# Layer 1 of a four-layer graph network: another order of the last block's turn, the partial products and the sums on TensorE and VectorE

## The chip, the cores and the metric

The kernel runs on one core of a Trainium2 chip. The metric is the device time of one execution in microseconds (us). Times of engines come from one profiled execution. The engines named here are PE (TensorE, matrix products; its weight loads are shown apart, as PEld), DVE (VectorE), ACT (ScalarE), POOL (GpSimd) and SP (SyncE, which issues the transfers). [...]

## The reference

A network with 512 nodes, 512 features and 16384 edges has four layers; each one normalises its input, cuts it at zero, and adds the layer's result to `x`:

```python
edge_index = jnp.stack([src, dst])
h = jnp.maximum(_layernorm(x, axis=-1), 0.0)
x = x + _L0_gnn_ref(h, edge_index, ...)      # attention over the graph, feed-forward
h = jnp.maximum(_layernorm(x, axis=-1), 0.0)
x = x + _L1_gnn_ref(h, L1_gnn_wc, L1_gnn_wn, L1_gnn_bias, edge_index)
h = jnp.maximum(_layernorm(x, axis=-1), 0.0)
x = x + _L2_gnn_ref(h, ...)                  # four experts of two layers, the best two per node
h = jnp.maximum(_layernorm(x, axis=-1), 0.0)
x = x + _L3_gnn_ref(h, edge_index, L3_gnn_W, L3_gnn_b)
```

The change lies in layer 1:

```python
alpha = x @ wc
beta = x @ wn
src, dst = (edge_index[0], edge_index[1])
sums = jax.ops.segment_sum(beta[dst], src, num_segments=x.shape[0])
counts = jax.ops.segment_sum(jnp.ones_like(src, dtype=beta.dtype), src, num_segments=x.shape[0])
gamma = sums / counts[:, None]
return alpha + gamma + bias
```

## The kernel before

The nodes are four blocks of 128 rows. The edges are counted into a 512 x 512 matrix once (`CT`, and `C` the other way round), so that a sum over neighbours is a matrix product with it. `xs` holds the residual stream, `h` the normalised rows, `hT` the same turned round. A *turn* of block b (`turn`, L189; `turn_pe`, L855) is four transposes on TensorE and one copy on ScalarE into `hT`.

Layer 1 (L870 to L974) does the following.

- *alpha*: `alpha_mm(b)` (L835) is four fp32 matmuls of 128 x 512 into the bank `pal`, which the profile shows as eight records. The function it returns adds the bank to `xs` on VectorE (L838). `add_bias1(b)` (L832) adds the bias to `xs` before it.
- *beta* = h · wn as a product of two 2 x 2 matrices of quarters with seven products instead of eight. `product(p, i, B)` (L778) is the i-th, four matmuls (eight records) of 128 x 256. Its operands are quarters of `hT` and `wns`, and sums of quarters that VectorE makes: `ls[0]` to `ls[3]` for `hT` (L749 to L752), `rb[0]` to `rb[3]` for `wns` (L759 to L762). Product 4 needs `ls[0]` and `rb[0]`, product 5 `ls[1]` and `rb[1]`, product 6 `ls[2]` and `rb[2]`, product 3 `rb[3]`, product 2 `ls[3]`; 0 and 1 need none, and no row of block 2 or 3.
- Three banks collect them: `pbe_a` takes products 0 and 1, `pbe_b` 5, 6 and 3, `pbe_c` 4 and 2. They go on adding into the same bank, and VectorE reads the state in between: `u2` after product 5, `u3` after 6, a third sum after 3 (all `plus`, L787, on L789). So product 6 can't start before `u2` has read `pbe_b`, nor product 3 before `u3` has.
- `beta_quarter` (L829) writes a quarter of beta as two parts: a rounded one by ScalarE (L726), and the rest by VectorE (`lo00` to `lo11`, L727).
- `gamma_mm(b)` (L840) is the sum over the neighbours, eight matmuls over the four blocks j of beta and its two parts; VectorE scales it and adds it to `xs` (L843). Then block b is normalised on VectorE and ScalarE (`gamma_begin`, `gamma_end`), turned, and used for the gates (`gates_mm`) and for layer 2's neighbour sums (`around_mm`, banks `pag`).
- `f0[0]` to `f0[7]` are VectorE's sums of the weights of layer 2's first expert (`wr0_0`, `wl0_0`).

The order on TensorE, VectorE and ScalarE is that of the code between L870 and L974: `manual_schedule` takes it as written. SP's queue of transfers isn't part of it; a load goes out when its place in the pool of five weight tiles is free. [...] a bank is given away again after the last use of what lay in it.

Of the kernel before, what the change touches and what calls it, by code (L numbers as in the profile page):

```python
# [22 lines left out]
NB = N // P  # L23
# [13 lines left out]
def fast(  # L37
# [4 lines left out]
    nc = tc.nc  # L42
# [11 lines left out]
    def bank(name):  # L54
        pool, tag = banks[taken[0] % len(banks)]
        taken[0] += 1
        return pool.tile([P, 512], F32, tag=tag, name=name)
# [73 lines left out]
    h = const.tile([P, NB, D], F32, name="h")  # L131
    hT = const.tile([P, KB, N], F32, name="hT")
# [46 lines left out]
    def norm_relu_end(blocks, name, begun, first=None):  # L179
        rs = rsqrt_end(*begun[1])  # L180
        for i, b in enumerate(blocks):
            nc.scalar.activation(h[:, b, :], begun[0][i], AF.Copy, scale=rs[:, i:i + 1])
            if first is not None:
                nc.scalar.activation(first, begun[0][i], AF.Copy, scale=rs[:, i:i + 1])
# [4 lines left out]
    def turn(dst_t, src_t, b, name):  # L189

        p = bank(f"tp_{name}{b}")
        for k in range(KB):
            nc.tensor.transpose(p[:, k * P:(k + 1) * P], src_t[:, b, k * P:(k + 1) * P], ident)
        nc.scalar.copy(dst_t[:, :, b * P:(b + 1) * P], p.rearrange("p (k n) -> p k n", k=KB))

    def mm(p, pairs):
        for i, (a, c) in enumerate(pairs):
            nc.tensor.matmul(p, a, c, start=(i == 0), stop=(i == len(pairs) - 1))  # L198

    def blk(t, k, j):  # L200
        return t[:, k, j * P:(j + 1) * P]
# [20 lines left out]
    CT = ct_p.tile([P, NB, N], R, name="CT")  # L222
# [187 lines left out]
    def ff_up_mm(hf, f):  # L410

        if f == 0:
            ffT[hf] = ffp.tile([P, FB, W], F32, tag="ffT", name=f"ffT{hf}")
        p = bank(f"pff{hf}_{f}").rearrange("p (i n) -> p i n", i=2)
        for i in range(2):
            mm(p[:, i, :], [(blk(w1[f // 4], k, (f + i) % 4), hT[:, k, hf * W:(hf + 1) * W]) for k in range(KB)])
        return p
# [26 lines left out]
    def norm2_c(b, begun):  # L444
        norm_relu_end((b,), "n1_", begun)
# [34 lines left out]
    with tc.manual_schedule(engines={ET.PE, ET.DVE, ET.Activation}):  # L480
# [25 lines left out]
        for c in range(NCH):  # L506
# [16 lines left out]
            i, at = divmod(c - 17, 9)  # L523
            if 0 <= i < len(first):
                w, t, off, j, cols = first[i]
# [98 lines left out]
        p = ff_up_mm(0, 2)  # L624
# [13 lines left out]
        p = ff_up_mm(0, 6)  # L638
# [39 lines left out]
        p = ff_up_mm(1, 0)  # L678
# [29 lines left out]
        p2, p3 = bank("pf22"), bank("pf23")  # L708
# [15 lines left out]
    def split_hi(hi, lo, full):  # L724

        nc.scalar.copy(hi, full)  # L726
        return lambda: nc.vector.tensor_sub(lo, full, hi.bitcast(F32))  # L727
# [26 lines left out]
    def right_steps(t, s, keep=None):  # L754

        b11, b12, b21, b22 = (quarter(t, i, j) for i in range(2) for j in range(2))
        last = b12 if keep is None else keep
        return (b11, b21, b22, s[:, 2], s[:, 0], s[:, 1], last), [
            lambda: nc.vector.tensor_sub(s[:, 0], b12, b11),  # L759
            lambda: nc.vector.tensor_sub(s[:, 1], b22, s[:, 0]),  # L760
            lambda: nc.vector.tensor_sub(last, b22, b12),
            lambda: nc.vector.tensor_sub(s[:, 2], b21, s[:, 1])]  # L762
# [9 lines left out]
    def right_sums(*a):  # L772
        return all_of(*right_steps(*a))

    def halves(name):
        return bank(name).rearrange("p (m n) -> p m n", m=2)

    def product(p, i, some, fresh=False):  # L778

        for m in range(2):  # L780
            for l, r in some:
                for k in range(2):
                    nc.tensor.matmul(p[:, m, :], l[i][:, k, m * P:(m + 1) * P], r[i][:, k, :], start=fresh,  # L783
                                     stop=(k == 1), skip_group_check=True)
                    fresh = False

    def plus(x, p, y=None):  # L787
        t = uu.tile([P, 2, W], F32, tag="u", name="u_sum") if y is None else y
        nc.vector.tensor_add(t, p, x)  # L789
        return t  # L790
# [21 lines left out]
    def sums_tile(name):  # L812
        return ws.tile([P, 3, 2, W], F32, tag="ws", name=f"ws_{name}")
# [12 lines left out]
    beta = pair.bitcast(R)  # L826
    hs = main.tile([P, 2, NB, D], R, tag="hs", name="hs")

    def beta_quarter(i, j, value):  # L829
        return split_hi(*(beta[:, g, 2 * i:2 * i + 2, j * W:(j + 1) * W] for g in range(2)), value)  # L830

    def add_bias1(b):  # L832
        nc.vector.tensor_add(xs[:, b, :], xs[:, b, :], bias1_b)

    def alpha_mm(b):  # L835
        p = bank(f"pal{b}")
        mm(p, [(blk(hT, k, b), wcs[:, k, :]) for k in range(KB)])
        return lambda: nc.vector.tensor_add(xs[:, b, :], p, xs[:, b, :])  # L838

    def gamma_mm(b):  # L840
        p = bank(f"psu{b}")
        mm(p, [(blk(CT, j, b), beta[:, i, j, :]) for j in range(NB) for i in range(2)])
        return lambda: nc.vector.scalar_tensor_tensor(xs[:, b, :], p, icnt[:, b:b + 1], xs[:, b, :],  # L843
                                                      op0=ALU.mult, op1=ALU.add)

    def gamma_begin(b):
        return norm_relu_begin((b,), "n2_")
# [22 lines left out]
    with tc.manual_schedule(engines={ET.PE, ET.DVE, ET.Activation}):  # L870
        RB, rb = right_steps(wns, sums_tile("wns"))
        ub, last = (uu.tile([P, 2, W], F32, tag="u", name=n) for n in ("u_first", "u_last"))
        L, ls = left_steps(hT, sums_tile("hT"), last)
        B = [(L, RB)]
        w0 = [load_w(src_w[0, 0], nm) for nm, src_w in (("wr0_0", Wr), ("wl0_0", Wl))]
        F0, f0 = zip(*(left_steps(w, sums_tile("w0")) for w in w0))
        f0 = [*f0[0], *f0[1]]
        ba = halves("pbe_a")
        product(ba, 0, B, True)
        nc.scalar.copy(ub, ba)  # L880
        a3 = norm2_a(3, y23)
        al = alpha_mm(0)
        turn(hT, h, 2, "h2_")
        n3 = norm2_b(3, *a3)
        al1 = alpha_mm(1)
        norm2_c(3, n3)
        product(ba, 1, B)
        lo00 = beta_quarter(0, 0, ba)
        add_bias1(0)
        al()  # L890
        rb[0]()
        al2 = alpha_mm(2)
        turn(hT, h, 3, "h2_")
        add_bias1(1)
        al1()
        ls[0]()
        rb[1]()
        ls[1]()
        bb, bc_ = halves("pbe_b"), halves("pbe_c")
        product(bc_, 4, B, True)  # L900
        product(bb, 5, B, True)
        rb[2]()
        ls[2]()
        rb[3]()
        ls[3]()
        add_bias1(2)
        al2()
        u2 = plus(ub, bb)
        product(bb, 6, B)
        lo00()  # L910
        f0[0]()
        u3 = plus(ub, bb)
        product(bb, 3, B)
        lo11 = beta_quarter(1, 1, plus(u3, bc_))
        product(bc_, 2, B)
        f0[1]()
        lo11()
        lo10 = beta_quarter(1, 0, plus(ub, bb))
        f0[2]()
        al3 = alpha_mm(3)  # L920
        lo10()
        lo01 = beta_quarter(0, 1, plus(u2, bc_))
        f0[3]()
        lo01()
        add_bias1(3)
        al3()
        for step in f0[4:6]:
            step()
        pg = bank("pg")
        pag = [bank(f"pag{k}") for k in range(KB)]  # L930
        psu = [gamma_mm(b) for b in range(3)]
        psu[0]()
        g0 = gamma_begin(0)
        psu[1]()
        gamma_end(0, g0)
        g1 = gamma_begin(1)
        cp = turn_pe(0)
        cp()
        psu.append(gamma_mm(3))
        psu[2]()  # L940
        gamma_end(1, g1)
        hs_low(0)
        gates_mm(0)
        g2 = gamma_begin(2)
        cp = turn_pe(1)
        cp()
        around_mm(0)
        psu[3]()
        gamma_end(2, g2)
        hs_low(1)  # L950
        gates_mm(1)
        g3 = gamma_begin(3)
        cp = turn_pe(2)
        cp()
        around_mm(1)
        f0[6]()
        gamma_end(3, g3)
        hs_low(2)
        cp = turn_pe(3)
        cp()  # L960
        f0[7]()
        hs_low(3)
        gates_mm(2)
        around_mm(2)
        gates_mm(3)
        around_mm(3)
        spair = main.tile([P, 2, NB, D], F32, tag="pair", name="sums")
        sums = spair.rearrange("p g s (k n) -> p g s k n", k=2)
        agT = main.tile([P, KB, N], F32, tag="agT", name="agT")
        XR = [right_sums(hT, sums[:, 0, 0:3], sums[:, 0, 3])]  # L970
        for k in range(KB):
            nc.vector.tensor_mul(agT[:, k, :], pag[k], ideg_b)
        XR.append(right_sums(agT, sums[:, 1, 0:3], sums[:, 1, 3]))
        F1 = weights0(1)  # L974
# [613 lines left out]
```

## Time and profile before

| | us |
|---|---|
| median of 3 runs | 522.12 (521.72 to 522.43) |
| the profiled execution | 524.05 |
| its span | 522.3 |
| TensorE busy in the span | 483.4 (93%) |
| VectorE busy | 367.7 (70%) |
| ScalarE busy | 156.9 (30%) |
| layer 1: the first product of beta starts | 208.84 |
| layer 1: the last turn of its input starts | 223.03 |
| layer 1: the last block of alpha starts | 239.88 |
| layer 1: the first neighbour sum is added on VectorE | 245.45 |
| layer 2: the first product starts | 265.11 |

By stage, busy us of each engine in the same execution:

| stretch, us | TensorE | VectorE | ScalarE | granted clock |
|---|---|---|---|---|
| 208.84 to 223.63 | 14.79 | 9.01 | 3.47 | 1.00 |
| 223.63 to 242.91 | 15.21 | 14.50 | 2.44 | 0.82 |
| 242.91 to 259.11 | 14.94 | 14.88 | 7.72 | 1.00 |
| 259.11 to 265.11 | 6.00 | 4.86 | 1.14 | 1.00 |

In an answer in order of time, a row has start and length, engine, line, operation, what is written and what is read (with sizes), how often, and in brackets for how long the engine stood idle before it and which instruction released it. Ends of matmuls are modelled and overlap by up to 0.2 us with the next start; from start to start is the better measure there. In a row by stretches, the numbers after the stretch are its length and then the busy time of PE, PEld, DVE, ACT and POOL, each with its count; the last three are the granted TensorE clock (1.00 is full), the share of the transfer engines, and GB/s.

### The profile page before, as it was taken

The numbers are of one execution on the slowest core, as the hardware profiler recorded it, in microseconds if no ns is written. First come the engines' busy times: TensorE is split into PE (matmuls) and PEld (weight loads), VectorE is DVE, ScalarE is ACT, GpSimd is POOL, SyncE is SP. The second block draws the span as 40 slices with busy tenths as digits, with TensorE's granted clock in tenths as the row PEclk, the third lists the DMA queues.
The fourth block names the chain that finished last, engine by engine and source line by source line (L and its number), as shares of the span: only waits on it lengthen the run. The fifth ranks groups of instructions, "written<-read, shape, count | busy, mean of one in ns | idle before, by whom it ended". The sixth has DMA issues, their size and how long they took to land.

```text
span 522.3 us, 5703 instructions
## 1 busy us (share of the span) xinstructions
PE 483.4 (93%) x2183; PEld 364.4 (70%) x2183; DVE 367.7 (70%) x744; ACT 156.9 (30%) x317; POOL 2.8 (1%) x10
## 2 busy tenths in 40 slices
PE   2999889697999999969999999999999999999995
PEld 1798556354774584547788888888888888885544
DVE  8898999998887784667993627851587135656652
ACT  3886344340531241201601122021112031122443
POOL 2000000000000000000000000000000000000000
PEclk9999999988999999988999999999999999999999
DMA  7810201200002133305000422220422040000002
GB/s 252 294 71 1 80 1 59 103 22 0 1 21 70 51 125 129 129 0 162 0 1 13 149 70 93 80 82 0 162 80 82 0 162 0 2 0 1 1 0 85
DMA packets 18497, 34.41 MB, mean 66 GB/s; under 512 B 1528, under 2 KB 2080, under 8 KB 18464
## 3 DMA queue, kind: packets, MB, share of 16 engines
q1 hardware_dynamic: 17504, 32.47, 18.4%
q10 hardware_dynamic: 960, 1.51, 0.8%
q8 instruction: 19, 0.31, 0.3%
q14 instruction: 14, 0.11, 0.1%
HBM read 32.93 MB, written 1.05 MB: 65 GB/s over the span
## 4 chain that ended last, share of the span: by engine, by line
PE 73%; DVE 20%; ACT 4%; issue 2%; DMA 0%; DVEq 0%; ACTq 0%
PE pe_b L783 8%; PE pff L198 5%; PE pe_a L783 5%; PE pf L430 5%; PE pe_c L783 5%; PE pq L198 5%; PE pz_b L783 3%; PE po_b L783 3%; PE pqk L198 3%; PE pwo L377 3%; PE pal L198 3%; PE ph L198 3%; PE cps L273 2%; DVE m L304 2%; PE po_c L783 2%; PE pz_c L783 2%
## 5 line engine op out<-in xcount | busy, mean ns | idle before, releaser
L789 DVE TENSOR_TENSOR u_sum<-pe_b,u_first 128x512 f32<-128x512 f32 x12 | 8.3, 692 | 50.8 <-PE pe_b L783 50.8
L198 PE MATMUL pq<-zz,C 128*128 128x512 f32 x128 | 32.8, 409 | 0.0
L271 DVE TENSOR_SCALAR ohs<-iota_h,src_f,dw_i 128x256 bf16<-128x256 f16 x104 | 28.9, 341 | 1.7 <-PE cps L273 1.6
L198 PE MATMUL pff<-hT,w 128*128 128x256 f32 x128 | 28.6, 381 | 0.4 <-issue 0.4
L273 PE MATMUL cps<-ohs,ohd 128*128 128x256 bf16 x104 | 19.7, 288 | 10.0 <-DVE ohs L271 10.0
L198 PEld LDWEIGHTS pq<-zz,C 128*128 128x128 f32 x128 | 24.0, 188 | 6.7 <-issue 1.2
L430 PE MATMUL pf<-w,ffT 128*128 128x512 f32 x64 | 28.1, 592 | 0.0
L1040 ACT ACTIVATE re<-te,gt 128x512 f32<-128x512 f32 x16 | 11.6, 724 | 54.9 <-DVE te L1038 54.9
L198 PEld LDWEIGHTS pff<-hT,w 128*128 128x128 f32 x128 | 24.1, 190 | 4.7 <-issue 1.4
L1002 ACT ACTIVATE eT<-u_sum,vecs 128x256 f32<-128x256 f32 x24 | 10.9, 500 | 52.9 <-DVE u_sum L789 52.9
L273 PEld LDWEIGHTS <-ohd 128*128 128x128 f16 x128 | 15.8, 145 | 14.1 <-DVE ohd L266 8.3
L430 PEld LDWEIGHTS pf<-w,ffT 128*128 128x128 f32 x64 | 11.9, 190 | 13.9 <-issue 13.9
L299 PE MATMUL psc<-qT,kT 64*128 64x256 f32 x128 | 17.6, 418 | 4.2 <-DVE s L310 4.2
L304 DVE TENSOR_REDUCE m<-psc 128x256 f32<-128x2048 f32 x8 | 18.3, 2287 | 1.2 <-PE cps L273 1.2
L310 DVE TENSOR_TENSOR s<-psc,m 128x1024 f32<-128x1024 f32 x16 | 18.8, 1216 | 0.1
L348 PE MATMUL aps<-s,v 128*64 128x256 f32 x128 | 16.1, 395 | 3.0 <-DVE nt_l L145 3.0
L726 ACT CAST zz<-u_sum 128x512 fp32r<-128x512 f32 x12 | 7.4, 618 | 37.7 <-DVE u_sum L789 37.7
L299 PEld LDWEIGHTS psc<-qT,kT 64*128 64x128 f32 x128 | 13.3, 204 | 7.8 <-issue 6.5
L338 DVE TENSOR_TENSOR s<-s,r 128x2048 f32<-128x2048 f32 x8 | 18.3, 2286 | 0.1
L311 ACT ACTIVATE s<-s 128x1024 f32<-128x1024 f32 x16 | 16.8, 1054 | 3.3 <-DVE s L310 2.9
L1041 DVE TENSOR_TENSOR xs<-xs,re 128x512 f32<-128x512 f32 x16 | 11.0, 690 | 9.3 <-ACT re L1040 9.3
L789 DVE TENSOR_TENSOR u_sum<-pz_b,u_first 128x512 f32<-128x512 f32 x12 | 8.3, 690 | 11.8 <-PE pz_b L783 11.6
(304 smaller groups left out, 1065.8 us busy)
## 6 DMA issues: line engine op xcount, KB each, us to landing
wr<-in_L_gnn_Wr_dram SPq DMA_DIRECT2D x8, 1024.0 KB
wl<-in_L_gnn_Wl_dram SPq DMA_DIRECT2D x8, 1024.0 KB
w<-in_L_gnn_W_dram SPq DMA_DIRECT2D x5, 1024.0 KB
wk<-in_L_gnn_Wk_dram SPq DMA_DIRECT2D x1, 1024.0 KB
wq<-in_L_gnn_Wq_dram ACTq DMA_DIRECT2D x1, 1024.0 KB
wv<-in_L_gnn_Wv_dram SPq DMA_DIRECT2D x1, 1024.0 KB
wo<-in_L_gnn_Wo_dram SPq DMA_DIRECT2D x1, 1024.0 KB
bl_b<-in_L_gnn_bl_dram SPq DMA_DIRECT2D x4, 256.0 KB
```

Of the source, the lines that this page charges most:

```text
L198: nc.tensor.matmul(p, a, c, start=(i == 0), stop=(i == len(pairs) - 1))
L271: nc.vector.tensor_scalar(ohs, iota_h, src_f[:, c:c + 1], dw_f[:, c:c + 1], op0=ALU.is_equal, op1=ALU.mult)
L273: nc.tensor.matmul(cps, ohd[0][:, :, c % 8], ohs, start=(c == 0), stop=(c == NCH - 1))
L299: nc.tensor.matmul(psc[i][:, 4 * g + j, :], kT[o:o + HD, j, b * P:(b + 1) * P], qT[o:o + HD, j, cols], start=True, stop=True)
L304: nc.vector.tensor_reduce(m, psc[i].rearrange("p h n -> p n h"), axis=AX.X, op=ALU.max)
L310: nc.vector.tensor_sub(s[:, g, :], psc[i][:, g, :], m[:, None, :].to_broadcast([P, 4, W]))
L311: nc.scalar.activation(s[:, g, :], s[:, g, :], AF.Exp, scale=1.0 / 8.0)
L338: nc.vector.tensor_mul(s, s, rz[i].to_broadcast([P, H, W]))
L348: nc.tensor.matmul(aps[hf][j // 2][o:o + HD, j % 2, :], v[:, b, (2 * j + g) * HD:(2 * j + g + 1) * HD], s[:, 4 * g + j, :], start=(b == 0 ...
L430: nc.tensor.matmul(p, ffT[b // 2][:, f, c:c + P], w2[f // 4][:, f % 4, :], start=(f == 0), stop=(f == FB - 1))
L783: nc.tensor.matmul(p[:, m, :], l[i][:, k, m * P:(m + 1) * P], r[i][:, k, :], start=fresh, stop=(k == 1), skip_group_check=True)
L789: nc.vector.tensor_add(t, p, x)
```

## The change

Layer 1's code gets another order; the same arithmetic is done.

- The turn of block 3 (`turn(hT, h, 3, ...)`) moves from behind product 1 and `alpha` block 2 to directly behind `alpha` block 1.
- `rb[0]` and `rb[1]` move ahead of the first bias and `alpha` sums; the sums of blocks 1 and 2 move later.
- Product 5 goes ahead of product 4, `ls[2]` ahead of `rb[2]`, and `rb[3]` and `ls[3]` behind `u2`.
- `alpha` block 2 moves from ahead of the turn to between products 6 and 3. Block 3 stays behind product 2.
- The weight sums `f0[0]` to `f0[3]` come later; `f0[3]` passes from ahead of to behind `alpha` 3's sum.
- `gamma_mm` can do some of the blocks j; the last neighbour sum is done in two halves, j = 0, 1 ahead of the turn of block 0 and j = 2, 3 behind it.

```diff
-    def gamma_mm(b):
-        p = bank(f"psu{b}")
-        mm(p, [(blk(CT, j, b), beta[:, i, j, :]) for j in range(NB) for i in range(2)])
+    def gamma_mm(b, p=None, some=range(NB)):
+        p = bank(f"psu{b}") if p is None else p
+        for j in some:
+            for i in range(2):
+                nc.tensor.matmul(p, blk(CT, j, b), beta[:, i, j, :], start=(j == 0 and i == 0),
+                                 stop=(j == NB - 1 and i == 1))
         return lambda: nc.vector.scalar_tensor_tensor(xs[:, b, :], p, icnt[:, b:b + 1], xs[:, b, :],
                                                       op0=ALU.mult, op1=ALU.add)
...
-        al = alpha_mm(0)
+        al = [alpha_mm(0)]
         turn(hT, h, 2, "h2_")
         n3 = norm2_b(3, *a3)
-        al1 = alpha_mm(1)
+        al.append(alpha_mm(1))
         norm2_c(3, n3)
+        turn(hT, h, 3, "h2_")
         product(ba, 1, B)
         lo00 = beta_quarter(0, 0, ba)
+        rb[0]()
+        rb[1]()
         add_bias1(0)
-        al()
-        rb[0]()
-        al2 = alpha_mm(2)
-        turn(hT, h, 3, "h2_")
-        add_bias1(1)
-        al1()
+        al[0]()
         ls[0]()
-        rb[1]()
         ls[1]()
         bb, bc_ = halves("pbe_b"), halves("pbe_c")
+        product(bb, 5, B, True)
         product(bc_, 4, B, True)
-        product(bb, 5, B, True)
+        ls[2]()
         rb[2]()
-        ls[2]()
+        u2 = plus(ub, bb)
+        product(bb, 6, B)
         rb[3]()
         ls[3]()
-        add_bias1(2)
-        al2()
-        u2 = plus(ub, bb)
-        product(bb, 6, B)
+        al.append(alpha_mm(2))
         lo00()
-        f0[0]()
+        add_bias1(1)
+        al[1]()
         u3 = plus(ub, bb)
         product(bb, 3, B)
         lo11 = beta_quarter(1, 1, plus(u3, bc_))
         product(bc_, 2, B)
+        add_bias1(2)
+        lo11()
+        al[2]()
+        f0[0]()
+        lo10 = beta_quarter(1, 0, plus(ub, bb))
         f0[1]()
-        lo11()
-        lo10 = beta_quarter(1, 0, plus(ub, bb))
-        f0[2]()
-        al3 = alpha_mm(3)
         lo10()
         lo01 = beta_quarter(0, 1, plus(u2, bc_))
-        f0[3]()
+        al.append(alpha_mm(3))
+        add_bias1(3)
         lo01()
-        add_bias1(3)
-        al3()
-        for step in f0[4:6]:
+        f0[2]()
+        al[3]()
+        for step in f0[3:6]:
             step()
         pg = bank("pg")
         pag = [bank(f"pag{k}") for k in range(KB)]
         psu = [gamma_mm(b) for b in range(3)]
+        p3 = bank("psu3")
+        psu.append(gamma_mm(3, p3, (0, 1)))
         psu[0]()
...
         cp = turn_pe(0)
         cp()
-        psu.append(gamma_mm(3))
+        gamma_mm(3, p3, (2, 3))
         psu[2]()
```

## The prediction

> **What bounds the kernel now.** I read the page's first two parts, then the busy time of each engine by stage, then the waits of this stage, its instructions in order of time, the chain that ended last, and the granted clock.
>
> TensorE is the engine that sets the end, and its clock row has a dip near the middle:
>
> ```profile
> span 522.3 us, 5703 instructions
> PE 483.4 (93%) x2183; PEld 364.4 (70%) x2183; DVE 367.7 (70%) x744; ACT 156.9 (30%) x317; POOL 2.8 (1%) x10
> PEclk9999999988999999988999999999999999999999
> ```
>
> Layer 1 is 208.84 to 265 us. From 265 to 480 TensorE is 96 to 100% busy in every 10 us, so whatever time `pe_a`, the first product of layer 2, gains at 265 the end should gain too. In layer 1 TensorE stands still in a few places. The waits of 205 to 265 us (time in all, times, longest):
>
> ```profile
> PE pbe_b L783 <- DVE u_sum L789: 2.7, 2, 1.9
> PE pbe_c L783 <- DVE ws_hT L749: 1.4, 1, 1.4
> PE tp_h L858 <- ACT h L182: 1.3, 2, 0.8
> ```
>
> The instructions in order of time (start, length, engine) show which work is late:
>
> ```profile
> 223.67 0.58 ACT L194 COPY hT<-tp_h 128x512 f32<-128x512 f32 x1 [3.29 <-PE tp_h L193]
> 224.29 0.69 DVE L749 TENSOR_TENSOR ws_hT<-hT 128x512 f32<-128x512 f32 x1 [4.56 <-ACT hT L194]
> 225.03 1.99 PE L783 MATMUL pbe_c<-ws_wns,ws_hT 128*128 128x256 f32 x8 [1.40 <-DVE ws_hT L749]
> ...
> 229.91 0.68 DVE L789 TENSOR_TENSOR u_sum<-pbe_b,u_first 128x512 f32<-128x512 f32 x1
> 230.64 3.06 PE L783 MATMUL pbe_b<-wns,u_last 128*128 128x256 f32 x8 [1.89 <-DVE u_sum L789]
> 233.74 0.69 DVE L789 TENSOR_TENSOR u_sum<-pbe_b,u_first 128x512 f32<-128x512 f32 x1 [1.96 <-PE pbe_b L783]
> 234.49 3.78 PE L783 MATMUL pbe_b<-ws_wns,hT 128*128 128x256 f32 x8 [0.78 <-DVE u_sum L789]
> 239.88 3.60 PE L198 MATMUL pal<-wcs,hT 128*128 128x512 f32 x8
> 243.51 0.69 DVE L838 TENSOR_TENSOR xs<-pal,xs 128x512 f32<-128x512 f32 x1 [0.56 <-PE pal L198]
> 245.45 0.75 DVE L843 SCALAR_TENSOR_TENSOR xs<-psu,icnt,xs 128x512 f32<-128x512 f32 x1
> ```
>
> First, VectorE sat idle 4.56 us until the last turn's copy, and then had ten sums to do at once; TensorE waited 1.40 us for the first (`ls[0]`), 1.89 us for `u2`, which reads the bank that product 6 is about to overwrite, and 0.78 us for `u3`. Second, two products of eight passes took 3.06 and 3.78 us, where their like take 1.89 (product 5 at 226.86). The granted clock, on a grid of 3.41 us laid so that it meets the edges of the clock's drops at 105.1, 125.6 and 231.4 us:
>
> ```profile
> 98.27:101.69 3.42, 1.54 (x12) 1.30 (x12) 3.35 (x5) 0.83 (x2) 0.00 (x0) 1.00 0.74 282
> ...
> 227.98:231.39 3.41, 1.52 (x7) 1.02 (x6) 3.31 (x7) 0.00 (x0) 0.00 (x0) 1.00 0.00 0
> 231.39:234.81 3.42, 2.64 (x7) 1.64 (x6) 1.43 (x3) 0.00 (x0) 0.00 (x0) 0.50 0.00 0
> 234.81:238.22 3.41, 3.41 (x9) 2.69 (x9) 1.64 (x3) 0.62 (x1) 0.00 (x0) 0.50 0.02 5
> ```
>
> (PE busy is the second number, PEclk the third from the right.) After a stretch with only 1.52 us of matmul the clock was halved for 6.8 us. Third, from 243.5 to 259.1 the chain that ended last runs on VectorE: the last `alpha` sum, two sums of layer 2's weights, then the four norms without a gap. There TensorE's waits (0.78 and 0.48 us) cost nothing.
>
> **The change part by part.** No instruction is added or removed on any engine, apart from the last neighbour sum's eight matmuls standing as four and four; SP's and POOL's queues keep their order. I therefore lay the new orders out with the old durations. TensorE, start to next start: a product 1.73 us, an `alpha` block 3.43, a turn 0.44, a neighbour sum 2.05 (6.14 for three). VectorE: a sum 0.60 behind an independent one, 0.72 if it reads the one before it, 0.79 for `add_bias1` to `alpha`. A product's result can be read 0.2 us after the next block starts (`pbe_a` at 217.87, its cast at 219.80).
>
> Last turn moved ahead. It stands behind `alpha` 1, at 217.87 instead of 223.03; its input `h` is written at 217.09, so it doesn't wait. Its copy ends at 219.09 (turn start +0.64, +0.58). Product 1 follows at 218.31 and needs no block of this turn. VectorE meanwhile does `rb[0]` 216.25, `rb[1]` 216.97, bias 217.57, `alpha` 0 218.36, and at 219.13 `ls[0]`, at 219.85 `ls[1]`, ready 220.54. Everything later on VectorE is queued behind that `ls[0]`, but it comes 5.2 us earlier than now. Product 5 now stands ahead of product 4 and needs `ls[1]`: TensorE, free at 220.04, starts it at 220.58, idle 0.54 us instead of 1.56 by starts.
>
> Blocks between the products. Product 5 220.58, product 4 222.31, product 6 224.04. `ls[2]` and `rb[2]` are done by 221.7, `u2` reads at 222.5 and is done by 223.2: 0.8 us spare under product 4. Now `alpha` 2 at 225.77, product 3 at 229.20: `u3` (226.3 to 227.0) has 2.2 us spare. Product 2 at 230.93 needs `ls[3]` (224.4) and the read of `pbe_c` (227.7). `alpha` 3 at 232.66, against 239.88 now: **7.22 us** earlier. That splits into 4.1 us of standing still plus clock: product 6 is read at 233.74 and would be at 230.64+1.93 = 232.57 (1.17), and product 3 took 3.57 to the next start instead of 1.73 (1.84), together 3.0; the rest is product 5's place and rounding.
>
> VectorE's order at the end. `alpha` 2's sum waits for its block (229.8) and holds up nothing needed before product 3's result at 231.1; the last split ends at 235.2, before `alpha` 3 ends (232.66+3.63 = 236.29), so the neighbour sums don't wait for it. But three weight sums, `f0[3]` to `f0[5]`, not two, now stand between `alpha` 3's sum and the first neighbour sum's: one more at **0.60 us**, and this is where VectorE is the bound. First neighbour sum on VectorE: 236.29+0.61+0.60+0.72+0.61 = 238.83, against 245.45: 6.62 earlier. Without that cover the sum that was moved would have been free: before, it stood in a wait.
>
> Last neighbour sum in halves. It fills the 0.78 us for which turn 0 waited, and turn 0 comes at most 0.25 us later than its input. What follows it (gates, `pag`) has 0.4 us more slack, but VectorE's norms set the pace: I cost it at 0, between −0.2 and +0.3. If VectorE were not the bound it would be worth up to 0.78. Its bank is the one `alpha` 1 left at 226, so no wait comes with it.
>
> Weight loads. The two loads that wait for `wns` and `wcs` go out 7 us earlier too (now 240.07 and 243.5), into a stretch with DMA share 0.00; their users are 25 us behind. 0.
>
> The sum: −7.22+0.60 = **−6.6 us**. The profiled execution took 524.05 us, span 522.3 and 1.75 around it: 517.4 with a span of 515.7. The median of the timed runs is 1.93 us under the profiled one; taken off it, 522.12−6.6 = **515.5 us**.
>
> [...] The longest gap here is 1.89. [...] By the row, 1.52 busy of 3.41 was enough, and in the new order no such stretch has more than about 0.6 us idle. I take the row. Its weakness: a stretch with 1.54 kept the clock (98.27), so the loss is at the edge, and [...] where it lies in another run no trace here shows.
>
> **The rivals.** (1) The timed runs before didn't lose the clock here, or only for one stretch. For it: that edge, and the 1.93 us by which they undercut the profiled run. Against it: 0.7 us between three runs, where a loss that came and went would spread them by 3. Gain 3.6 (518.5), or with one stretch of half rate (3.41/2 = 1.7) 5.3 (516.8). (2) VectorE is late and takes TensorE's place: from 216.25 to the first neighbour sum it has 31 operations, about 20.2 us, of 22.6. If each took 0.05 more, product 6 or the split would slip by 0.5 to 1: 516.3. (3) Slower: the half clock moves and stays. If `ls[1]` came 1.4 us later than laid out, the gap ahead of product 5 would reach 1.9; then half rate costs 1.7 us in every 3.41, and with 2.64 busy of 3.42 not having restored it (231.39), the gappy stretch up to 253 might not either. It decides from (6.6+1.0)/1.7 = 4.5 such stretches, 15 us: 523.2. (4) No change: VectorE's order eats it all, needing 6 us of waits against 2.4 of its slack.
>
> **How the numbers follow.** The laid-out order 0.58 (515.5, own range 514.7 to 516.7); rival 1 0.33, two thirds of it at 518.5; rival 2 0.05 beyond that; rivals 3 and 4 0.04. The range 514.6 to 519.0 leaves out rivals 3 and 4 and the tails. A measurement here tells 0.2% (1.0 us) from no change: faster 0.95, same 0.03, slower 0.02.
>
> **What would show it.** Right: turn 3 at 217.9, product 5 at about 220.6 after a wait under 0.8 us, every product 1.9 us, clock 1.00 from 216 to 260, no wait of TensorE for `u_sum`, the first neighbour sum on VectorE 2.5 us behind `alpha` 3's sum (now 1.94), `pe_a` at 258.5, all of layer 2 shifted alike. Wrong: a half clock at another place of layer 1, a wait for `u_sum` ahead of product 6, or VectorE idle over 0.5 us behind `alpha` 3.

## The result and the profile after

The changed kernel takes 518.33 us (median of 4 runs, 517.71 to 518.67), against 522.14 before: ratio 0.9926, 95% interval 0.9909 to 0.9943. That is 3.8 us less, where 6.6 were forecast (515.5). It lies in the stated range, beside the 518.5 of rival 1. The profiled execution of the changed kernel took 518.36 us with a span of 516.5.

Its page, the clock row:

```profile
span 516.5 us, 5702 instructions
PEclk9999999979999999999999999999999999999998
```

The dip in the middle is gone: the granted clock is 1.00 in all of layer 1 (209.19 to 258.94 us). The waits of 205 to 260 us in which TensorE stood still (total, times, longest):

```profile
PE tp_h L861 <- ACT h L182: 1.4, 3, 0.7
...
PE pbe_b L783 <- DVE ws_hT L750: 0.4, 1, 0.4
```

No wait for `u_sum` is left; one of 0.4 us for `ls[1]` is new. The same stage in order of time (start, length, engine, line):

```profile
218.22 0.60 PE L193 MATMUL tp_h<-ident,h 128*128 128x128 f32 x4
...
220.94 1.99 PE L783 MATMUL pbe_b<-ws_wns,ws_hT 128*128 128x256 f32 x8 [0.40 <-DVE ws_hT L750]
222.98 0.69 DVE L789 TENSOR_TENSOR u_sum<-pbe_b,u_first 128x512 f32<-128x512 f32 x1 [0.88 <-PE pbe_b L783]
224.50 1.89 PE L783 MATMUL pbe_b<-wns,u_last 128*128 128x256 f32 x8
226.23 3.60 PE L198 MATMUL pal<-wcs,hT 128*128 128x512 f32 x8
229.66 1.89 PE L783 MATMUL pbe_b<-ws_wns,hT 128*128 128x256 f32 x8
...
233.12 3.60 PE L198 MATMUL pal<-wcs,hT 128*128 128x512 f32 x8
236.15 7.08 PE L844 MATMUL psu<-pair,CT 128*128 128x512 f32 x28
236.75 0.69 DVE L838 TENSOR_TENSOR xs<-pal,xs 128x512 f32<-128x512 f32 x1 [0.52 <-PE pal L198]
...
239.28 0.74 DVE L846 SCALAR_TENSOR_TENSOR xs<-psu,icnt,xs 128x512 f32<-128x512 f32 x1
...
258.94 1.89 PE L783 MATMUL pe_a<-hT,wr 128*128 128x256 f32 x8
```

Layer 1 begins 0.35 us later in this execution (209.19). With that taken off, the order laid out beforehand is met to 0.11 us: the turn at 217.87, product 5 at 220.59 (laid out 220.58), `alpha` 3 at 232.77 (232.66), the first neighbour sum added at 238.93 (238.83). From the first product of beta (209.19) to layer 2's first product (258.94), below called "layer 1", it is 49.75 us instead of 56.27 in the profile before: 6.5 us less. So the layout was right, and yet the timed runs gained only 3.8. What was to be found out is where the other 2.8 us are.

### The profile page after: what moved, and what is told of

Its sections match the earlier page's. It is cut to its first block, busy times and chain, and to the rows that moved or that the text cites. A ratio compares the mean times of both kernels' runs of the same rounds, so it can differ in the third digit from the quotient of the medians.

```text
span 516.5 us, 5702 instructions
## 1 busy us (share of the span) xinstructions
PE 480.8 (93%) x2183; PEld 362.6 (70%) x2183; DVE 367.9 (71%) x744; ACT 156.8 (30%) x317; POOL 2.8 (1%) x10
## 3 DMA queue, kind: packets, MB, share of 16 engines
HBM read 32.93 MB, written 1.05 MB: 66 GB/s over the span
## 4 chain that ended last, share of the span: by engine, by line
PE 74%; DVE 18%; ACT 3%; DMA 2%; issue 2%; SPq 0%; ACTq 0%; DVEq 0%
PE pe_b L783 8%; PE pff L198 5%; PE pe_a L783 5%; PE pf L430 5%; PE pe_c L783 5%; PE pq L198 5%; PE pz_b L783 3%; PE pqk L198 3%; PE po_b L783 3%; PE pwo L377 3%; PE pal L198 3%; PE ph L198 3%; PE cps L273 2%; DVE m L304 2%; PE po_a L783 2%; PE pz_a L783 2%
```

## The experiments

"Theory 1" is the prediction's: the kernel before lost TensorE's clock in layer 1 in its timed runs too. "Theory 2" is rival 1: they kept it.

**The kernel before once more** (no edit).

> The kernel before, unchanged, to see where other executions of it stand. Theory 1 (the clock is lost in layer 1 in every execution, and the profiled one was longer for another reason): a profile with half clock near 231 to 238 us again, a mean granted clock of about 0.986 in the timed runs too, spans near 520.3. Theory 2 (the timed executions keep the clock in layer 1; the profiled one was one that lost it): no half clock between 216 and 260 us, product 3 in 1.9 us instead of 3.8, mean granted clock near 0.992, span about 3 us under 522.3 less what other stretches lose.

Measured: 521.19 us (12 runs, 520.50 to 522.14), every run with a mean granted clock of 0.990 or 0.991. Layer 1 took 53.36 us in its profile (209.44 to 262.80). Its instructions in order of time:

```profile
231.24 1.99 PE L783 MATMUL pbe_b<-wns,u_last 128*128 128x256 f32 x8 [1.88 <-DVE u_sum L789]
...
234.01 1.99 PE L783 MATMUL pbe_b<-ws_wns,hT 128*128 128x256 f32 x8 [0.78 <-DVE u_sum L789]
...
262.80 1.89 PE L783 MATMUL pe_a<-hT,wr 128*128 128x256 f32 x8
```

The same waits, 1.88 and 0.78 us, but products 6 and 3 take 1.99 us each where the profile shown before had 3.06 and 3.78. The half clock cost 56.27−53.36 = 2.9 us there, as sized (3.0), but that execution wasn't a typical one. The kernel before also ran beside the experiments, 64 times in three series, and these runs fall into two groups by their mean granted clock. 45 runs have 0.990 or 0.991 and a median of 521.70 us (520.66 to 522.66), 19 have 0.982 to 0.986 and 524.57 us (522.81 to 525.24). Both groups stand in each series (9 of 28, 8 of 29 and 2 of 7 are of the second). The profile before had 0.986 and 524.05. Theory 2 holds: the few timed runs that the prediction started from were, by their times, of the first group, the profile of the second. A mean clock doesn't tell where it was lost; that it was layer 1 rests on the two profiles, whose layer 1 differs by the same 2.9 us as the two medians.

Of the 12 runs here none is of the second group, nor of the four beside the result, so it is 19 of 80 on record. The ratio of these 12 runs to the 28 beside them is 0.9978 [0.9960, 0.9997], although nothing was edited: the share of the second group alone makes such a difference.

**Idle matmuls in the longest wait**, in the kernel before:

```diff
         u2 = plus(ub, bb)
+        idle = bank("idle")
+        for n in range(6):
+            nc.tensor.matmul(idle, blk(CT, 0, 0), C[:, 0, :], start=True, stop=True)
         product(bb, 6, B)
```

> The kernel before, with six idle matmuls of 128x512 (0.25 us each, 1.5 us in all, into a bank that nobody reads) on TensorE in the 1.89 us in which it waits ahead of product 6. No order is changed. Theory 1: the clock stays whole and product 6, product 3 and product 2 get 3.0 us back: about 519.1. Theory 2: there was nothing to lose in most runs: 522.1, within 0.5.

Measured: 521.69 us (12 runs, 521.19 to 522.46), ratio 0.9989 [0.9969, 1.0009]; layer 1 53.36 us, TensorE's wait 0.50 instead of 1.88:

```profile
231.13 1.99 PE L783 MATMUL pbe_b<-wns,u_last 128*128 128x256 f32 x8 [0.50 <-DVE u_sum L789]
```

That is theory 2's number: filling this wait returned nothing in runs that keep the clock. None of the 12 runs had a time of the second group, but neither had any of the 12 unedited ones above, so whether the filling also prevents the loss isn't shown by the times. The profiles give a hint, no more: wherever a stretch of 3.41 us (as long as the half clock from 105.10 lasted in the profile before) is laid in layer 1, it has at least 2.01 us of matmul here, and down to 1.53 in the unedited kernel's profile above; in the profile before, the half clock followed a stretch with 1.52.

**A longer wait**, in the kernel before:

```diff
         al2()
+        rb[3]()
+        ls[3]()
         u2 = plus(ub, bb)
```

> The kernel before with rb[3] and ls[3] computed twice (1.2 us on VectorE, same result) ahead of u2, so that TensorE waits 3.1 us instead of 1.9 ahead of product 6. Theory 2 with a clock that falls when some 1.9 us of a 3.4 us stretch are idle, wherever the stretches lie: four of five runs lose the clock, about 525.6 (1.2 for the wait, 3.0 for the clock), the rest 522.6. [...]

Measured: 524.67 us (20 runs, 522.98 to 525.54), ratio 1.0038 [1.0024, 1.0053]. 13 of 20 runs have a clock of 0.983 to 0.986 (median 524.96), 7 have 0.989 to 0.992 (523.36). With the kernel before it was 19 of 64. With a gap of 3.09 us a larger share of the runs has the lower clock than with one of 1.89, and not all have it, as theory 2 said (it had four runs of five; 13 of 20 were measured). The sizes came out less cleanly: the two groups lie 1.6 us apart, not 3.0, and the slower one is only 0.4 above that of the unlengthened kernel although its profile has exactly the added 1.2 us (57.47 against 56.27). Why isn't settled.

Three profiles can be laid on a grid of 3.41 us that meets the edges of each one's own clock drops: in the profile before they last 3.41 us from 105.10 and from 125.58, and 6.83 from 231.39; in the kernel before once more 6.8 from 104.5; in the longer wait 6.83 from 233.12. The profile before stood in the prediction (1.52 us busy, lost). First comes the kernel before once more, then the longer wait (PE busy is the second number, the clock the third from the right):

```profile
227.34:230.75 3.41, 2.01 (x10) 1.43 (x8) 3.31 (x7) 0.00 (x0) 0.00 (x0) 1.00 0.00 0
230.75:234.17 3.42, 2.15 (x9) 1.59 (x10) 2.50 (x5) 0.00 (x0) 0.00 (x0) 1.00 0.00 0
```

```profile
229.71:233.12 3.41, 1.45 (x7) 1.30 (x8) 3.10 (x6) 0.00 (x0) 0.00 (x0) 1.00 0.00 0
233.12:236.53 3.41, 2.63 (x7) 1.64 (x6) 2.30 (x4) 0.62 (x1) 0.00 (x0) 0.50 0.02 5
236.53:239.95 3.42, 3.42 (x9) 2.71 (x9) 1.65 (x3) 0.55 (x1) 0.00 (x0) 0.50 0.00 0
```

In the first the boundary at 230.75 cuts the wait of 1.88 us (229.4 to 231.2) into 1.4 and 0.5; neither stretch falls under 2 us busy, and the clock stays. In the second a stretch has 1.45 us busy, the clock is 0.50 from its end on, still 0.50 behind the next with 2.63 busy, and 1.00 again behind the one with 3.42. In the kernel's first profile the boundary was at 231.39, so the whole wait (228.75 to 230.64) fell into one stretch. So the same code, with the same wait (1.88 and 1.89 us), kept its clock in one execution and lost it in another, and the grid lay differently in the two. That the one follows from the other is my reading of these profiles; they don't prove it.

**Only the turn moved**, in the kernel before:

```diff
         norm2_c(3, n3)
+        turn(hT, h, 3, "h2_")
         product(ba, 1, B)
 ...
         al2 = alpha_mm(2)
-        turn(hT, h, 3, "h2_")
         add_bias1(1)
```

> The kernel before with only the last turn moved, directly behind alpha block 1; every other instruction in its old order. Laid out with the old durations: the 1.56 us ahead of product 4 go, the eleven sums behind the copy come early, so that product 6 waits 0.9 us for u2 instead of 1.9, product 3 waits 0.95 for u3: alpha 3 starts 3.0 us earlier, layer 1 50.4 us, and no single stretch of 3.4 us is more than 1.9 idle, so no run loses the clock: 518.5, in one group. The rival, that the whole block between the half products is the larger part: layer 1 52 us or more, 520.

Measured: 519.08 us (4 runs, 518.46 to 519.37), ratio 0.9947 [0.9929, 0.9964], all in one group (four runs are too few to show that none is ever lost); layer 1 50.6 us. In order of time:

```profile
223.50 1.89 PE L783 MATMUL pbe_c<-ws_wns,ws_hT 128*128 128x256 f32 x8
...
227.90 1.99 PE L783 MATMUL pbe_b<-wns,u_last 128*128 128x256 f32 x8 [0.78 <-DVE u_sum L789]
...
230.68 1.99 PE L783 MATMUL pbe_b<-ws_wns,hT 128*128 128x256 f32 x8 [0.79 <-DVE u_sum L789]
```

Product 4 no longer waits, `u2` costs 0.78 us instead of 1.88. Moving the turn alone makes 2.8 of the 3.6 us by which layer 1 gets shorter when the clock is kept (53.36 to 50.59, and to 49.75 with the whole change). All the rest of the change adds 0.8.

**The block back in front of the half products**, in the changed kernel:

```diff
         lo00 = beta_quarter(0, 0, ba)
+        al.append(alpha_mm(2))
         rb[0]()
 ...
         ls[3]()
-        al.append(alpha_mm(2))
         lo00()
```

> The changed kernel with alpha block 2 back in front of the half products, behind product 1, all else as changed. By the laid-out order it then covers the wait for ls[1] (0.5 us back) and product 3 waits 0.9 us for u3: layer 1 50.1 us, 0.4 slower than the changed kernel. If the whole block between the half products is what gave the gain: up to 2 us slower.

Measured: 519.10 us (6 runs, 518.59 to 519.23); layer 1 50.95 us, 1.2 longer than the changed kernel's, where 0.4 was expected.

```profile
229.58 1.99 PE L783 MATMUL pbe_b<-ws_wns,hT 128*128 128x256 f32 x8 [1.05 <-DVE u_sum L789]
...
236.70 0.69 DVE L751 TENSOR_TENSOR wr<-wr 128x512 f32<-128x512 f32 x1
237.31 0.68 DVE L838 TENSOR_TENSOR xs<-pal,xs 128x512 f32<-128x512 f32 x1
```

Product 3's wait is as laid out (1.05 against 0.9). What I had missed is VectorE: until product 5's result it now stands idle for 3.65 us, and then it has no pause any more up to the neighbour sums. `f0[2]` at 236.70 pushes the last `alpha` sum 1.14 us behind the start of the neighbour sums (236.17), where it was 0.60. Of the 1.2 us, 0.66 come before the neighbour sums, where TensorE waits for `u3` (1.05, less the 0.40 that it no longer waits for `ls[1]`), and 0.54 behind their start, where VectorE is late. The whole block between the half products is worth that much, because VectorE's sums then lie under it.

**`f0[3]` back ahead of the last `alpha` sum**, in the changed kernel:

```diff
         f0[2]()
+        f0[3]()
         al[3]()
-        for step in f0[3:6]:
+        for step in f0[4:6]:
             step()
```

> The changed kernel with one weight sum, f0[3], put back ahead of the last alpha block's sum, where VectorE waited 0.5 us. My sum of the change costed its move at 0.60 us on the chain that sets the end: 517.8 (0.5 to 0.6 below 518.3) if the norms on VectorE set the pace there, 518.3 if TensorE does.

Measured: 517.65 us (5 runs, 516.81 to 518.47). The times alone don't separate it from the changed kernel (517.79 in its longer series below), but the profile does: the first neighbour sum is added 2.54 us behind the start of the neighbour sums instead of 3.13, and layer 1 takes 49.14 us instead of 49.75. That is the 0.60 us that the prediction charged for moving it.

**The last neighbour sum whole**, in the changed kernel:

```diff
-        p3 = bank("psu3")
-        psu.append(gamma_mm(3, p3, (0, 1)))
 ...
         cp = turn_pe(0)
         cp()
-        gamma_mm(3, p3, (2, 3))
+        psu.append(gamma_mm(3))
```

> The changed kernel with the last neighbour sum whole again, behind the turn of block 0. If VectorE's norms set the pace, as I costed it: 518.3, within 0.3. If the halves are worth what TensorE waited ahead of that turn: up to 0.8 us slower, 519.1.

Measured: 517.78 us (8 runs, 517.16 to 519.40); layer 1 49.75 us, the same as with the halves. The wait that the halves had filled is back, and larger:

```profile
242.89 0.65 PE L861 MATMUL tp_h<-ident,h 128*128 128x128 f32 x4 [1.38 <-ACT h L182]
```

1.38 us of TensorE's idle time cost nothing here: VectorE's norms set the pace. This part of the change is worth zero.

**A version with layer 2's weight sums out of the way**, from the changed kernel:

```diff
         f0[2]()
+        f0[3]()
         al[3]()
-        for step in f0[3:6]:
-            step()
 ...
         around_mm(1)
-        f0[6]()
+        f0[4]()
 ...
-        f0[7]()
+        f0[5]()
 ...
         XR = [right_sums(hT, sums[:, 0, 0:3], sums[:, 0, 3])]
+        f0[6]()
+        f0[7]()
```

> The changed kernel with layer 2's weight sums out of the way of layer 1's norms: f0[3] ahead of the last alpha sum, f0[4] and f0[5] where f0[6] and f0[7] stood, f0[6] and f0[7] behind layer 2's first four sums of hT. If VectorE sets the pace from the last alpha sum on: the first neighbour sum is added as soon as TensorE has it, 2.25 us behind the start of the neighbour sums instead of 3.13, so 0.9 us less, 517.4, layer 1 48.8 us. If the moved sums come back as waits of layer 2: 518.3.

Measured: 517.34 us (6 runs, 516.68 to 517.61), ratio 0.9890 [0.9862, 0.9917]; layer 1 49.10 us.

```profile
236.72 0.68 DVE L838 TENSOR_TENSOR xs<-pal,xs 128x512 f32<-128x512 f32 x1
238.57 0.75 DVE L846 SCALAR_TENSOR_TENSOR xs<-psu,icnt,xs 128x512 f32<-128x512 f32 x1 [1.17 <-PE psu L844]
```

VectorE now waits 1.17 us for TensorE, whose first neighbour sum can be read 2.46 us behind its start, not 2.25 as I had reckoned. So moving `f0[4]` and `f0[5]` as well brings 0.04 us more than moving `f0[3]` alone. It is the lowest median of the study, 0.45 us under the changed kernel in the same series, but that is 0.09%, less than these runs can separate. Two of its six runs have a mean clock of 0.986 and are no slower for it (517.33 and 517.34), so a lower mean clock went without lost time here.

**The changed kernel once more** (no edit).

> The changed kernel, unchanged, for a comparison with many runs. Theory 2: the change gives back 3.7 us of standing still less queueing (layer 1 from its first product to that of layer 2: 49.7 us in the profile of the changed kernel, 53.4 in the profile of the kernel before that kept its clock), and 6.5 against those runs of before that lost it. Spread of the changed kernel under 2 us, with nothing near its median plus 3, while before has two groups 3 us apart.

Measured: 517.79 us (6 runs, 517.34 to 518.04), all with a clock of 0.991 or 0.992, ratio 0.9903 [0.9875, 0.9930]; layer 1 49.77 us. Against the kernel before where it kept its clock that is 521.70−517.79 = 3.9 us, against its other runs 6.8.

## Why the prediction was off in size and right in kind

Right, by its own steps:

- *The turn moved ahead* and *the blocks between the products*: product 5 to `alpha` 3 came within 0.11 us of the layout, and the new wait ahead of product 5 was 0.4 us by the profile (0.55 by starts, 0.54 laid out).
- *`f0[3]` at 0.60 us*, with VectorE as the bound: measured 0.61 by putting it back.
- *The halves at 0*: measured 0.00 in layer 1.
- *3.0 us for the half clock*: measured 2.9 between two profiles of the kernel before.

Wrong is the last step of the sum: "The median of the timed runs is 1.93 us under the profiled one; taken off it, 522.12−6.6". That treated the 1.93 us as a constant that lies over both kernels. It was not: the profiled execution had lost the clock in layer 1 and the timed ones hadn't. In the changed kernel the profiled execution lies 0.03 us over the median, not 1.93. The step that failed is therefore the clock's 3.0 us as a gain of the timed runs, where it is nothing. Of the three points weighed, the two for rival 1 (the edge, and the 1.93 us) were right and got too little weight. The one against it decided nothing: three runs that keep the clock agree to 0.7 us as well as three that lose it. Had the 3.0 us been left out of the sum, it would have given 3.6, and 518.5 against the measured 518.33. The chance of 0.33 for the rival, and of 0.58 for the laid-out order with a loss in every run, should have been the other way round. That the time lies in the range is owed to the part given to rival 1; the layout's own range, 514.7 to 516.7, missed it.

The row that the prediction took was right in kind: behind a stretch with 1.52 us busy the clock was halved, and behind one with 1.45 in the longer wait. Wrong was to take one execution's grid for that of all. With gaps of 1.89 and 3.09 us the lower clock stands in 19 of 64 and in 13 of 20 runs, and in the two profiles of the kernel before, the boundary by the wait lies 22.55 us behind the start of layer 1 in the one and 21.31 in the other.

Rival 2 (VectorE late) didn't happen in the changed kernel; with the block put back in front of the half products it did, at 1.2 us in all. Rivals 3 and 4 didn't happen.

The two spans differ by 5.8 us, layer 1 by 6.5. Of the rest, 0.35 lies ahead of layer 1, where the clock drops fell differently (two of 3.41 us before, from 105.10 and 125.58; one of 6.8 after, from 104.1), and 0.37 behind it. Each is within what two executions of one kernel differ by there (layer 1 starts at 208.4 to 209.8 us over the profiles), and neither was looked into.

## What to carry to other kernels

Where a profile shows a reduced clock, compare the profiled execution's time with the timed runs before its cost goes into a sum: a profile that is 1.6 us longer than the slowest of them (524.05 against 522.43) may be one of the executions that lost it (19 of 64 had the lower clock here), and the difference between two profiles then contains the luck of one. When a producer late on one engine makes a burst on another, moving the producer ahead can be worth most of what a full reordering brings (2.8 of 3.6 us here). Fill a wait only where the waiting engine sets the end: 1.38 us of idle TensorE ahead of a turn cost nothing, while one sum of 0.60 us moved into VectorE's chain cost all of its 0.60.

## What the runs showed of the hardware

In the profile before, the granted clock of TensorE fell from 1.00 to 0.50 at 231.39 us, behind a stretch of 3.41 us with 1.52 us of matmul in it (227.98 to 231.39); in that of the longer wait it fell at 233.12, behind one with 1.45 (229.71 to 233.12). It stayed at 1.00 behind a stretch with 1.54 us in the profile before (98.27 to 101.69), and behind two with 2.01 and 2.15 in the kernel before once more (227.34 to 230.75 and 230.75 to 234.17). It was still 0.50 behind stretches with 2.64 us busy (before, 231.39 to 234.81) and 2.63 (the longer wait, 233.12 to 236.53), and 1.00 again behind the next ones with 3.41 and 3.42, from 238.22 and 239.95. These are the stretches of three executions; what the clock does in others they don't show.

One and the same kernel has two groups of times 2.9 us apart (45 runs at 521.70, 19 at 524.57). One profile of each group is at hand, and in them the wait of 1.89 us lies differently to the grid. In layer 1 of the changed kernel no stretch of 3.41 us, wherever it begins, has less than 2.68 us of matmul. That fits the narrow spread of its ten runs, which lie within 1.3 us (517.34 to 518.67). The prediction didn't count that as a gain, and the median doesn't show it.
